# A two-layer graph network on one core: the last expert layer in gapless tiles and visits, and the loop for stray edges moved behind its gates

## The chip, the cores and the metric

The kernel runs on one core of a Trainium2 chip. The time is the device time of one execution in microseconds (us); lower is better. Engines are named as in the profile: PE does matrix products (PEld is its weight load), DVE is the vector engine, ACT the scalar engine, POOL the general engine, whose queue also issues the indirect DMAs (gathers and scatters by a list of row numbers), and SP issues most plain DMAs. Each engine works through its own list of instructions in order and waits for the others by semaphores. DMA transfers run beside them.

## The reference

2500 tokens of 256 values, 40,000 edges, two layers. Each layer adds a graph convolution and an attention part to x and then a mixture of experts. What the change touches is the last step of the second layer:

```python
def _L1_ffn_ref(x, W1, b1, Wg, bg, Wd, bd):        # W1 256x1024, Wg 1024x8, Wd 8x1024x256
    H = gelu(x @ W1 + b1)                            # 2500 x 1024
    probs = softmax(H @ Wg + bg)                     # 2500 x 8
    assign = argmax(probs)
    for e in range(8):
        y = H @ Wd[e] + bd[e]
        out = out + where(assign == e, probs[:, e:e+1] * y, 0)
    return out
...
x = x + gcn(xn, edges) + mix(xn)                     # two convolutions over the edges
x = x + _L1_ffn_ref(layernorm(x), ...)
```

The hidden layer H is the same for all experts. It decides which expert a token belongs to, and only the down-projection Wd differs from expert to expert. Each token goes through one expert alone.

## The kernel before

Tokens lie in X as 20 tiles of 125 rows (X[p, k, :]), five groups of four tiles. A row of X has 256 values and four more: mean, inverse deviation, probability of the chosen expert, and number of the token.

*Convolutions.* The adjacency is written to DRAM once (adj) and is read back in pieces of 219 KB, one hundred over both convolutions, `conv_1` and `conv_2`, through four buffers, all issued by SP in order. For each group, `neighbours` (L288) multiplies 120 times on PE; `conv_2` then transposes the sums (L898) and adds them to X (L901).

*Stray edges.* The adjacency is built for a bounded number of edges per row block. What does not fit would be handled by `lost1`, a loop that runs n_lost times, 0 or 1, known only at run time. On these inputs its body is not run. It stands between conv_2 and the last expert layer, and since it can change X, what reads X comes after it. All five engines meet at it.

*Last expert layer.* Weights (wgf, bgf, b1f, w1, and wd in eight loads of 1 MB) are issued by SP, bdf by ACT. `layernorm_T` computes the statistics of a group (L328 and following), the normalised rows lnt (L361) and their transpose xT (L348). `gates` computes H of the group in eight chunks (L1198), gelu on ACT (L1201) and the logits (L1202); H is then dropped. `route` makes softmax and the chosen expert of each token. `take_slots` gives each token a row in DRAM: every expert has a region of CAP rows in sorted1, fill1 counts how far it is filled. `scatter` (L403) writes the rows of X there, one indirect DMA per tile. The routing of a group is worked off while the next group's chunks run.

After the last group `pad` (L491) writes a tile of empty rows behind each expert's region, and `plan` works out for up to NS1 = 27 tiles of 128 rows which expert they belong to and where they begin. 27 is the number of full tiles in 2500 rows, 20, plus one part tile for seven of the eight experts. Then nine groups of three tiles follow: SP loads the rows (L1243) from an address in a register, DVE normalises (L1247), PE transposes (L1251), DVE and ACT copy to xc (L90, L92), PE computes the hidden layer again on 3456 columns in all (L1257), ACT does gelu (L1259), and for each tile PE multiplies with the expert's wd (L1265, eight calls; the expert's number is a register load, L445). DVE adds the bias (L1269), scales and adds the row (L1270), and POOL writes the rows to out by token number (L1271). Rows that belong to no token have a number out of bounds and are not written.

The order of instructions on an engine is made by a scheduler from the program's order and its dependences, so the order in the code is not always that on the engine.

Of the kernel before, what the change touches and what calls it, by code (L numbers as in the profile page):

```python
# [9 lines left out]
F32 = mybir.dt.float32  # L10
I32 = mybir.dt.int32
# [5 lines left out]
N = 2500  # L17
# [22 lines left out]
NS1 = -(-N // TS) + NE - 1  # L40
# [8 lines left out]
def gps_kernel(ctx: ExitStack, tc: tile.TileContext, a, out):  # L49
# [23 lines left out]
    def mm_tile(p, n):  # L73
        return psum.tile([p, n], F32, tag="mm", name="mm")

    def row_bcast(src, offset, n, p=P):
        return bass.AP(tensor=src.tensor, offset=src.offset + offset, ap=[[0, p], [1, n]])
# [8 lines left out]
    def evacuate(dst, src):  # L86

        flip[0] ^= 1
        if flip[0]:
            S.copy(dst, src)  # L90
        else:
            V.tensor_copy(dst, src)  # L92


    X = xpool.tile([P, NT, RW], F32, tag="X", name="X")
# [25 lines left out]
    slots = const.tile([P, NS0], F32, name="slots")  # L121
# [4 lines left out]
    region = const.tile([P, NE], F32, name="region")  # L126
# [252 lines left out]
    def take_slots(pool, mask, fill):  # L379


        flat = mask.rearrange("p i e -> p (i e)")
        ps = psum2.tile([P, 2, GT, NE], F32, tag="cx", name="ps")
        T.matmul(ps[:, 0].rearrange("p i e -> p (i e)"), below, flat, start=True, stop=True)  # L384
        T.matmul(ps[:, 1].rearrange("p i e -> p (i e)"), ones[:, :P], flat, start=True, stop=True)  # L385
        slot = pool.tile([P, GT, NE], F32, tag="slot", name="slot", bufs=2)
        for k in range(GT):
            V.tensor_tensor(slot[:, k, :], ps[:, 0, k, :], fill, ALU.add)  # L388
            V.tensor_tensor(fill, ps[:, 1, k, :], fill, ALU.add)
        return slot  # L390
# [19 lines left out]
    def plan(pool, fill, ns):  # L410
# [3 lines left out]
        V.tensor_tensor(tiles, fill, region, ALU.subtract)  # L414
# [7 lines left out]
        V.tensor_tensor(of, last[:, None, :].to_broadcast([P, ns, NE]), slots[:, :ns, None].to_broadcast([P, ns, NE]), ALU.is_le)  # L422
# [6 lines left out]
        V.scalar_tensor_tensor(tiles, tiles, -float(TS), region, ALU.mult, ALU.add)  # L429
# [4 lines left out]
        V.scalar_tensor_tensor(who, slots[:, :ns], float(TS), who, ALU.mult, ALU.add)  # L434
        begin = pool.tile([P, ns], I32, name="begin")
        V.tensor_scalar(begin, who, float(NE * CAP), None, ALU.min)
        return expert, begin

# [38 lines left out]
    sorted1 = dram.tile([NE * CAP + TS, RW], F32, name="sorted1")  # L477
    back0 = dram.tile([2 * N, D], F32, name="back0")

    for table in (sorted0, sorted1):  # L480
        nc.scalar.dma_start(table[NE * CAP:NE * CAP + TS, :], empty)

    def pad(pool, table, empty, fill, moved):

        ends = pool.tile([P, NE], I32, name="ends")
        V.tensor_copy(ends, fill)
        made = []
        for e in range(NE):
            r = nc.values_load(ends[0:1, e:e + 1], engines=[mybir.EngineType.SP], min_val=0, max_val=NE * CAP - TS,
                               skip_runtime_bounds_check_because="an expert has at most N tokens")  # L490
            made.append(nc.sync.dma_start(table[ds(r, TS), :], empty))  # L491
            for m in moved + made[:-1]:
                tc.declare_no_dep(made[-1].ins, m.ins, reason="rows of their own")
# [5 lines left out]
    fill0 = const.tile([P, NE], F32, name="fill0")  # L499
    V.tensor_copy(fill0, region)  # L500
    fill1 = const.tile([P, NE], F32, name="fill1")
    V.tensor_copy(fill1, region)
# [633 lines left out]
    with tc.tile_pool(name="lost1", bufs=1) as pool, tc.For_i(0, n_lost, 1):  # L1136
        acc = pool.tile([P, NT, D + 1], F32, name="acc")
        nc.sync.dma_start(acc[:, :, :D], tab1.rearrange("(p k) d -> p k d", p=P))
        V.memset(acc[:, :, D:], 0.0)
        gather_sums(pool, acc, tab1)  # L1140
        tab2 = dram.tile([N, D], F32, name="tab2")
        brow = pool.tile([P, D], F32, name="brow")
        nc.sync.dma_start(brow, row_bcast(a["b1row"], 0, D))
        cT = pool.tile([128, 2, N], F32, name="cT")
        for i in range(NT):
            o = acc[:, i, :D]
            V.scalar_tensor_tensor(o, o, dis[:, i:i + 1], brow, ALU.mult, ALU.add)
            neg = pool.tile([P, D], F32, name="neg")
            V.tensor_scalar(neg, o, 0.0, alpha[:P], ALU.min, ALU.mult)
            V.scalar_tensor_tensor(o, o, 0.0, neg, ALU.max, ALU.add)  # L1150
        for g in range(NG):
            transpose_group(cT, g, lambda k: acc[:, g * GT + k, :D])
        for i in range(NT):
            ps = mm_tile(P, D)
            for c in range(2):
                T.matmul(ps, cT[:, c, i * P:(i + 1) * P], wc2[:, c, :], start=(c == 0), stop=(c == 1))
            V.tensor_scalar(acc[:, i, :D], ps, dis[:, i:i + 1], None, ALU.mult)
        nc.sync.dma_start(tab2.rearrange("(p k) d -> p k d", p=P), acc[:, :, :D])
        gather_sums(pool, acc, tab2)
        for i in range(NT):  # L1160
            V.scalar_tensor_tensor(X[:, i, :D], acc[:, i, :D], dis[:, i:i + 1], X[:, i, :D], ALU.mult, ALU.add)

# [4 lines left out]
    TG = 3  # L1167
    with tc.tile_pool(name="fin", bufs=1) as fin, tc.tile_pool(name="fin2", bufs=2) as fin2:
# [13 lines left out]
        xT = fin.tile([128, 2, N], F32, name="xTf")  # L1182
# [6 lines left out]
        empty = empty_rows(fin)  # L1189
# [17 lines left out]
        def route(g, pl):  # L1207
# [18 lines left out]
            slot = take_slots(fin2, w, fill1)  # L1226
            scatter(sorted1, slot_of(fin2, slot, w), X[:, g * GT:(g + 1) * GT, :], moved)
            yield

        layernorm_T(X, xT, lambda g: fin2.tile([P, GT, D], F32, tag="lnt", name="lnt"), stats=with_row, then=gates)  # L1230
        for _ in range(2):
            next(routing[-1])
        pad(fin, sorted1, empty, fill1, moved)
        expert, begin = plan(fin, fill1, NS1)

        ns = -(-NS1 // TG) * TG
        done = []
        for u in range(ns // TG):
            tiles = range(u * TG, min((u + 1) * TG, NS1))
            nt = len(tiles)  # L1240
            xs = fin2.tile([128, TG, RW], F32, tag="xs", name="xs")
            for k, t in enumerate(tiles):
                nc.sync.dma_start(xs[:, k, :], tile_rows(sorted1, begin, t))  # L1243
            xc = fin2.tile([128, 2, TG * TS], F32, tag="xc", name="xc")
            xh = fin2.tile([128, TG, D], F32, tag="xh", name="xh", bufs=1)
            for k in range(nt):
                V.tensor_scalar(xh[:, k, :], xs[:, k, :D], xs[:, k, D:D + 1], xs[:, k, D + 1:D + 2], ALU.subtract, ALU.mult)  # L1247
            for c in range(2):
                ps = mm_tile(128, TG * TS)
                for k in range(nt):  # L1250
                    T.transpose(ps[:, k * TS:(k + 1) * TS], xh[:, k, c * 128:(c + 1) * 128], ident)  # L1251
                evacuate(xc[:, c, :nt * TS], ps[:, :nt * TS])
            hs = []
            for j in range(nj):
                ps = mm_tile(128, TG * TS)
                for c in range(2):
                    T.matmul(ps[:, :nt * TS], w1[:, c, j * 128:(j + 1) * 128], xc[:, c, :nt * TS], start=(c == 0), stop=(c == 1))  # L1257
                h = fin2.tile([128, TG * TS], F32, tag="hs", name="hs", bufs=12)
                S.activation(h[:, :nt * TS], ps[:, :nt * TS], AF.Gelu, bias=b1f[:, j:j + 1])  # L1259
                hs.append(h)  # L1260
            for k, t in enumerate(tiles):
                e = expert_of(expert, t)
                ps = mm_tile(128, D)
                for j in range(nj):
                    T.matmul(ps, hs[j][:, k * TS:(k + 1) * TS], wd[:, ds(e, 1), j, :], start=(j == 0), stop=(j == nj - 1))  # L1265
                idx = fin2.tile([128, 1], I32, tag="idx", name="idx", bufs=4)
                V.tensor_copy(idx, xs[:, k, D + 3:D + 4])
                yo = fin2.tile([128, D], F32, tag="yo", name="yo", bufs=4)
                V.tensor_tensor(yo, ps, bdf[:, ds(e, 1), :].rearrange("p o n -> p (o n)"), ALU.add)  # L1269
                V.scalar_tensor_tensor(yo, yo, xs[:, k, D + 2:D + 3], xs[:, k, :D], ALU.mult, ALU.add)  # L1270
                done.append(G.indirect_dma_start(  # L1271
                    out=out, out_offset=bass.IndirectOffsetOnAxis(ap=idx, axis=0), in_=yo, in_offset=None,
                    bounds_check=N - 1, oob_is_err=False,
                ))
                for m in done[:-1]:
                    tc.declare_no_dep(done[-1].ins, m.ins, reason="each token has a slot of its own")
# [62 lines left out]
```

## Time and profile before

| what | before |
|---|---|
| median of 3 runs | 2235.64 us (2235.45 to 2235.82) |
| the profiled execution | 2239.74 us, of which its span 2238.0 us |
| PE busy | 2009.1 us, 90% |
| DVE, ACT, POOL busy | 872.0, 594.2, 294.4 us |
| last conv_2 group's products end | 1860.98 us |
| gates, first L1198 to last L1202 | 1877.68 to 1998.51 us |
| last token's row in sorted1 known (L398) | 2005.83 us |
| tiles of experts on PE (L1257 to L1265) | 2022.33 to 2230.45 us |

In the lines of the profile, a group is given as line, engine, operation, output and inputs, shape, and number of instructions, then busy time, mean nanoseconds of one, and the idle time ahead of it with what ended it. In the timeline, the first number is the start in us, the second the length, and in brackets stands how long the engine had been idle and what released it. A row of the slices has one digit for each fortieth of the span, the busy share in tenths.

### The profile page before, as it was taken

What the parts mean: (1) busy time and instruction counts of PE and PEld (TensorE: products, weight loads), DVE (VectorE), ACT (ScalarE), POOL (GpSimd) and SP (SyncE); (2) the same over time, 40 slices, a digit from 0 to 9 for tenths busy, and PEclk for the clock granted to TensorE, in tenths of its full rate; (3) what the DMA queues carried; (4) which work ended last, traced back from release to release, by engine and by line L of the source; (5) the groups of instructions that cost most, each with busy time, mean ns of one, the idle gap of its engine ahead of it and who ended that gap; (6) DMA issues with size and microseconds to landing.
All of it is one profiled execution on the core that took longest, in us unless ns stands there. A gap on an engine that the chain in (4) does not pass through costs nothing. (4 is left out here: it accounts for less than half of the span.)

```text
span 2238.0 us, 25483 instructions
## 1 busy us (share of the span) xinstructions
PE 2009.1 (90%) x9145; PEld 1336.2 (60%) x9145; DVE 872.0 (39%) x2764; ACT 594.2 (27%) x1008; POOL 294.4 (13%) x265
## 2 busy tenths in 40 slices
PE   2799956997799999999999999999987997978998
PEld 2556635876476766676666676767643442326676
DVE  7866532332734463434525463443120003222111
ACT  1533202222533323232233324133110001332221
POOL 2303331222210000100001010011111000120111
PEclk9799977999899999999999999999989998988999
DMA  4113256664410001100110001100025336011110
GB/s 119 37 55 105 78 155 188 206 188 152 105 51 14 1 12 51 42 1 5 45 35 23 1 12 49 47 1 1 1 75 152 86 90 203 19 42 38 31 30 20
DMA packets 87295, 143.51 MB, mean 64 GB/s; under 512 B 18898, under 2 KB 69056, under 8 KB 86402
## 3 DMA queue, kind: packets, MB, share of 16 engines
q1 hardware_dynamic: 71233, 117.01, 18.0%
q0 software_dynamic: 12832, 18.28, 2.9%
q10 hardware_dynamic: 3093, 6.46, 1.1%
q8 instruction: 77, 1.26, 0.2%
q14 instruction: 60, 0.49, 0.1%
HBM read 104.84 MB, written 38.81 MB: 64 GB/s over the span
## 5 line engine op out<-in xcount | busy, mean ns | idle before, releaser
L1089 PE MATMUL mm<-w,h 128*125 128x256 f32 x1280 | 286.1, 379 | 0.0
L1079 PE MATMUL mm<-xT,w 128*128 128x500 f32 x640 | 283.2, 584 | 0.0
L288 PE MATMUL pa<-piece,table 125*128 125x500 bf16 x1200 | 269.8, 378 | 13.5 <-DVE t L852 5.6
L1089 PEld LDWEIGHTS mm<-w,h 128*125 128x125 f32 x1280 | 239.0, 188 | 43.2 <-issue 9.2
L288 PEld LDWEIGHTS <-table 125*128 125x128 bf16 x1200 | 117.7, 99 | 144.5 <-issue 17.8
L1079 PEld LDWEIGHTS mm<-xT,w 128*128 128x128 f32 x640 | 119.3, 191 | 112.6 <-issue 102.2
L1082 ACT ACTIVATE h<-mm,bf 128x500 f32<-128x500 f32 x160 | 107.1, 677 | 231.5 <-PE mm L1079 231.1
L288 PE MATMUL pa<-edges,xb 125*128 125x500 bf16 x600 | 134.2, 377 | 1.7 <-ACT edges L662 1.7
L1074 POOL TENSOR_TENSOR tok<-tok,b 125x1024 f32<-125x1024 f32 x20 | 47.3, 2365 | 584.6 <-DVE tok L1066 534.1
L1090 DVE TENSOR_TENSOR tok<-tok,mm 125x256 f32<-125x256 f32 x80 | 33.5, 418 | 210.0 <-PE mm L1089 169.3
L1257 PE MATMUL mm<-xc,w 128*128 128x384 f32 x288 | 102.1, 511 | 7.5 <-DVE xc L92 5.4
L765 PE MATMUL mm<-xc,wt 128*128 128x128 f32 x752 | 97.1, 283 | 7.5 <-DVE idx L771 4.3
L765 PEld LDWEIGHTS mm<-xc,wt 128*128 128x128 f32 x752 | 89.6, 194 | 17.8 <-DVE xc L761 12.4
L779 PE MATMUL py<-w,h 128*128 x376 | 96.0, 381 | 0.9 <-ACT h L769 0.9
L288 PEld LDWEIGHTS <-xb 125*128 125x128 bf16 x600 | 58.1, 100 | 63.8 <-issue 3.9
L1265 PE MATMUL mm<-wd,hs 128*128 x432 | 94.7, 379 | 0.0
L1055 DVE TENSOR_TENSOR tok<-tok,po 125x256 f32<-125x256 f32 x80 | 30.2, 414 | 154.4 <-PE po L1052 153.9
L769 ACT ACTIVATE h<-mm,wt 128x128 f32<-128x128 f32 x188 | 53.8, 368 | 137.3 <-issue 127.1
L1265 PEld LDWEIGHTS mm<-wd,hs 128*128 128x128 f32 x432 | 82.1, 190 | 13.1
L353 ACT ACTIVATE xT<-mm,mixc 128x500 f32<-128x500 f32 x80 | 58.9, 767 | 114.0 <-PE mm L348 79.8
L662 ACT CAST edges<-mm 125x500 bf16<-125x500 f32 x100 | 64.6, 784 | 88.9 <-PE mm L659 88.9
L1257 PEld LDWEIGHTS mm<-xc,w 128*128 128x128 f32 x288 | 55.4, 198 | 50.9 <-DVE xc L92 10.8
(325 smaller groups left out, 2832.2 us busy)
## 6 DMA issues: line engine op xcount, KB each, us to landing
wt<-in_expert_in_dram SPq DMA_DIRECT2D x47, 514.0 KB
piece<-adj SPq DMA_DIRECT2D x100, 218.8 KB
xs<-sorted SPq DMA_DIRECT2D x74, 130.0 KB
w<-in_L_mix_W_dram SPq DMA_DIRECT2D x8, 1024.0 KB
wd<-in_L_ffn_Wd_dram SPq DMA_DIRECT2D x8, 1024.0 KB
w<-in_L_ffn_W_dram SPq DMA_DIRECT2D x8, 512.0 KB
adj<-edges SPq DMA_DIRECT2D x2, 1750.0 KB
terms<-t SPq DMA_DIRECT2D x10, 336.0 KB
```

The lines of the kernel that those rows point to most:

```text
L288: T.matmul(pa[c], table[:, k, n, c * 128:(c + 1) * 128], e, start=(k == 0 and n == 0), stop=(k == NT - 1 and n == 2))
L353: S.activation(o, ps, AF.Identity, bias=shift[:, c:c + 1], scale=gain[:, c:c + 1])
L662: S.copy(o.rearrange("p s (n d) -> p n s d", d=BD), ps[:P].rearrange("p (n s d) -> p n s d", n=BD, d=BD))
L765: T.matmul(ps[:, j * TS:(j + 1) * TS], wt[:, c * F0 + j * 128:c * F0 + (j + 1) * 128], xc[:, c * TS:(c + 1) * TS], start=(c == 0), stop=(c ...
L769: S.activation(h[:, j * TS:(j + 1) * TS], ps[:, j * TS:(j + 1) * TS], AF.Gelu, bias=wt[:, 2 * F0 + j:2 * F0 + j + 1])
L779: T.matmul(ps, h[:, j * TS:(j + 1) * TS], w2[:, ds(e, 1), j, :], start=(j == 0), stop=(j == NJ - 1))
L1074: G.tensor_tensor(o, o, b2[:P, None, :].to_broadcast([P, GT, D]), ALU.add)
L1079: T.matmul(ps, w1[:, c, j * 128:(j + 1) * 128], fT[:, c, g * GC:(g + 1) * GC], start=(c == 0), stop=(c == 1))
L1082: S.activation(h, ps, AF.Gelu, bias=bf[:, l, j:j + 1])
L1089: T.matmul(ps, hh[j][:, k * P:(k + 1) * P], w2[:, j, :], start=(j == 0), stop=(j == nj - 1))
L1257: T.matmul(ps[:, :nt * TS], w1[:, c, j * 128:(j + 1) * 128], xc[:, c, :nt * TS], start=(c == 0), stop=(c == 1))
L1265: T.matmul(ps, hs[j][:, k * TS:(k + 1) * TS], wd[:, ds(e, 1), j, :], start=(j == 0), stop=(j == nj - 1))
```

## The change

*Gapless tiles.* A token's row is no longer in a region of its expert's own. Two neighbouring experts share N rows: one fills them from the front, the other from the back (begin1, sign, way). sorted1 now lies in the memory of adj, which has been read for the last time by then. `visits` on DVE computes, for 20 gapless tiles of 128 in the order of experts, the row of each place (whence), and for 27 visits the expert, the tile (which), and the tile's place in a ring (kept). A visit is one tile with one expert; a tile in which an expert ends is visited more than once. `fetch` gathers the rows of a tile on POOL into X itself, `turned` normalises and transposes them, `inner` computes the hidden layer of a group of two or four tiles (2500 columns in all) and stores it in a ring of 12 tiles. For each visit, `take` copies the tile's hidden layer (128×1024) from the ring at an address in a register, and `visit` multiplies with the expert's wd. Rows of the tile that belong to another expert get a token number out of bounds (far). `pad` and the row loads on SP go.

*The loop.* `lost1` stands behind the gates. Its body now ends with `sort_all`, which does norm, gates and sort once more, for X has changed.

```diff
-    with tc.tile_pool(name="lost1", bufs=1) as pool, tc.For_i(0, n_lost, 1):
-        ...
     stage.close()
...
-        layernorm_T(X, xT, lambda g: ..., stats=with_row, then=gates)
-        for _ in range(2):
-            next(routing[-1])
-        pad(fin, sorted1, empty, fill1, moved)
-        expert, begin = plan(fin, fill1, NS1)
+        def sort_all():
+            V.tensor_copy(fill1, begin1.rearrange("p k t -> p (k t)"))
+            moved.append([])
+            routing.clear()
+            layernorm_T(X, xT, lambda g: ..., stats=with_row, then=gates)
+            for _ in range(2):
+                next(routing[-1])
+
+        sort_all()
+        with tc.tile_pool(name="lost1", bufs=1) as pool, tc.For_i(0, n_lost, 1):
+            ...
+            sort_all()
+        own, whence, expert, expert_f, which, kept = visits(fin, fill1, at)
...
+            way = fin2.tile([P, GT, NE], F32, tag="way", name="way")
+            V.tensor_tensor(way, w, sign..., ALU.mult)
-            slot = take_slots(fin2, w, fill1)
+            slot = take_slots(fin2, way, fill1)
...
-        for u in range(ns // TG):
-            for k, t in enumerate(tiles):
-                nc.sync.dma_start(xs[:, k, :], tile_rows(sorted1, begin, t))
-            ...
+        hs = fin2.tile([128, RING, nj * TS], F32, name="hs", bufs=1)
+        xs = whole
+        for n in (2, 2, 4, 4, 4, 4):
+            ...
+        def fetch(lo, hi):
+            for t in range(lo, hi):
+                G.indirect_dma_start(out=xs[:m, t, :], out_offset=None, in_=sorted1,
+                    in_offset=bass.IndirectOffsetOnAxis(ap=whence[:m, t:t + 1], axis=0))
+        def take(v):
+            r = nc.values_load(kept[0:1, v:v + 1], engines=[mybir.EngineType.DVE], ...)
+            h = fin2.tile([128, nj * TS], F32, tag="taken", name="taken")
+            V.tensor_copy(h, hs[:, ds(r, 1), :].rearrange("p o n -> p (o n)"))
+            return v, h
+        def visit(v, h):
+            e = expert_of(expert, v)
+            r = nc.values_load(which[0:1, v:v + 1], engines=[mybir.EngineType.DVE], ...)
+            for j in range(nj):
+                T.matmul(ps, h[:, j * TS:(j + 1) * TS], wd[:, ds(e, 1), j, :], ...)
+            row = xs[:, ds(r, 1), :].rearrange("p o n -> p (o n)")
+            V.tensor_scalar(far, own[:, ds(r, 1)], expert_f[:, v:v + 1], float(1 << 20), ALU.not_equal, ALU.mult)
+            V.tensor_tensor(idx, far, row[:, D + 3:D + 4], ALU.add)
+            V.tensor_tensor(yo, ps, bdf[:, ds(e, 1), :]..., ALU.add)
+            V.scalar_tensor_tensor(yo, yo, row[:, D + 2:D + 3], row[:, :D], ALU.mult, ALU.add)
+            G.indirect_dma_start(out=out, ..., in_=yo)
+        fetch(*groups[0])
+        fetch(*groups[1])
+        xc, n = turned(*groups[0])
+        taken = None
+        for u, (lo, hi) in enumerate(groups):
+            inner(lo, hi, xc, n)
+            for v in range(lo, hi if u + 1 < len(groups) else NV):
+                nxt_v = take(v)
+                if taken is not None:
+                    visit(*taken)
+                taken = nxt_v
+                if v == lo and u + 1 < len(groups):
+                    xc, n = turned(*groups[u + 1])
+            if u + 2 < len(groups):
+                fetch(*groups[u + 2])
+        visit(*taken)
```

In the new program the lines have moved: pa is L292, conv_2's transposes and sums L961 and L964, the gates L1237, L1240 and L1241, norm and lnt L332 and L365, the loop L1282, scatter L407, the slots' row numbers L402, fetch L1328, xh L1340, its transposes L1342, inner L1353, gelu L1355, take L1364 and L1367, visit L1373 to L1386.

In the instructions that the scheduler made of it, the norm statistics and lnt of earlier groups stand on DVE between conv_2's groups, and eight lnt transposes and seven of the eighty L1237 products stand on PE there. The weight loads of the last layer (wgf, bgf, b1f, w1, wd, bdf) have left their place behind the loop; on SP they stand in conv_1, between piece loads 32 and 44. On PE, a group's hidden layer, part of the visits and the transposes of the next group but one take turns, and the last twelve visits follow each other.

## The prediction

> **What bounds the kernel now.** First the page's busy shares and slices, then its costliest groups. PE is busy 90% of a span of 2238.0 us, so what counts is where PE stands still and what it does that it need not. The last slices are the stages that the change touches (a slice is 56 us).
>
> ```profile
> PE 2009.1 (90%) x9145; PEld 1336.2 (60%) x9145; DVE 872.0 (39%) x2764; ACT 594.2 (27%) x1008; POOL 294.4 (13%) x265
> ...
> PE   2799956997799999999999999999987997978998
> ...
> L1257 PE MATMUL mm<-xc,w 128*128 128x384 f32 x288 | 102.1, 511 | 7.5 <-DVE xc L92 5.4
> ...
> L1265 PE MATMUL mm<-wd,hs 128*128 x432 | 94.7, 379 | 0.0
> ```
>
> See that the expert stage is PE's own time: 102 us of hidden layer, 95 us of down-projection, 7.5 us of waits between.
>
> Next the timeline around the loop for stray edges, which runs no iteration here.
>
> ```profile
> 1861.81 1.03 PE L898 MATMUL ps<-ident,u 128*125 128x128 f32 x7 [0.38 <-DVE u L92]
> 1862.44 1.66 DVE L901 SCALAR_TENSOR_TENSOR X<-ps,dval,X 125x256 f32<-125x256 f32 x4 [0.69 <-PE ps L898]
> ...
> 1868.70 0.28 DVE L470 MEMSET empty<- 128x260 f32 x1 [4.60 <-issue]
> ...
> 1875.13 1.36 DVE L361 TENSOR_SCALAR lnt<-X,mv,rstd 125x256 f32<-125x256 f32 x4
> ...
> 1875.58 2.06 PE L348 MATMUL mm<-ident,lnt 125*128 125x125 f32 x8 [12.75 <-DVE lnt L361]
> ```
>
> PE stands 12.75 us: DVE is held 4.60 us at the loop, then needs 6.9 us of norm statistics that nothing could start before the loop.
>
> The same view between gates and experts, in three fragments: last logits, last slots and scatters, first hidden tile.
>
> ```profile
> 1997.51 1.00 PE L1202 MATMUL pl<-h,wgf 128*8 128x500 f32 x2 [0.83 <-ACT h L1201]
> ...
> 2005.64 0.19 DVE L398 TENSOR_REDUCE to<-pick 125x4 int32<-125x32 f32 x1
> ...
> 2006.12 1.19 POOL L403 DMA_INDIRECT sorted<-X,to  x1 [7.32 <-DVE tiles L416]
> ...
> 2019.42 0.47 PE L1251 MATMUL mm<-ident,xh 128*128 128x128 f32 x1 [15.63 <-DVE xh L1247]
> ...
> 2022.33 3.93 PE L1257 MATMUL mm<-xc,w 128*128 128x384 f32 x6
> ```
>
> From the last slot (2005.83) to the first hidden matmul is 16.5 us. And one group of three tiles:
>
> ```profile
> 2047.52 9.94 PE L1257 MATMUL mm<-xc,w 128*128 128x384 f32 x30 [0.71 <-DVE xc L92]
> 2057.30 10.52 PE L1265 MATMUL mm<-wd,hs 128*128 x48
> 2067.66 0.82 PE L1251 MATMUL mm<-ident,xh 128*128 128x128 f32 x6
> ```
>
> Fifteen calls (two records each) of 384 columns in 9.94 us are 1.726 ns a column; 24 calls of 256 columns in 10.52 us are 1.712. The stage runs 2022.33 to 2230.45, 208.1 us, and 7.55 us of last output follow.
>
> **The change, part by part.**
>
> *1. The loop leaves the place between conv_2 and gates.* Norm statistics and lnt of the earlier groups now stand between conv_2's groups on DVE, which is idle there while PE does a 25.5 us group (L288); cost nothing, and if that cover failed, the 6.9 us return. In the built order, eight lnt transposes and seven of the eighty L1198 calls also go inside conv_2's four boundaries. A boundary is 2.39 us of which PE works 1.4; what is put in exceeds its idle 1.0 us by 1.05, .75 and .75 us (the fourth nothing), so the last pa ends 1863.5 instead of 1860.98. After it come the last transposes, X (1.66 us) and one lnt group, partly under a remaining L1198; gates resume about 1866.6 with seven calls done (5.9 us at 0.84). Before, gates ran 1877.68 to 1998.51 = 120.8 us; now the end is 1866.6 + 120.8 − 5.9 = 1981.5. The tail to the last slot was 7.3 us, plus .2 for the multiply by the sign: 1989.0 against 2005.83. **Gain 16.8.**
>
> *2. The weight loads.* wgf, b1f, w1 and eight wd (10.5 MB) stood on SP behind the loop. They now go out in conv_1 (about 1625 to 1700 us), between piece loads 32 and 44 of 100 and ahead of term stores. A wd issue cost 2.9 us of SP (four in 11.46), twelve pieces last 30 us on PE (ten per 25.5 us group), and 13 MB in all at the 350 GB/s seen when wd was loaded (1866 to 1876) need 37. Four piece buffers cover 10. Nothing to 8 us; I take 1.5, since 37 − 30 is within the cover.
>
> *3. Start of the experts.* After the last slot: four scatters, 6.1 us as before (2005.83 to 2011.9). Then the loop's barrier waits for them to land. The nearest row is the first loop of the kernel, also behind scatters: last scatter issued 336.38, DVE back 341.40, 5.0 us. Then the new table of visits: 33 small DVE ops, .16 to .38 us each in the rows of the old plan, 7.3 us (the old plan lay under scatters and padding). Then the first gather of rows on POOL: the nearest row, the 125-row gather at L184, took 4.1 us from issue to use; the second 1.5 later. xh, transposes and copies 1.4. Sum 6.1 + 5.0 + 7.3 + 5.6 + 1.5 = 25.5 against 16.5: **loss 9.0.** The padding DMAs (L491, 8.66 us of SP) and the first xs loads go with the old 16.5.
>
> Here a rule speaks against the move. The Trainium skill, "Runtime: NRT & Kernel Launch", section "Instruction fetch mechanics", says that a branch taken to code outside the fetched window stops the engine until a page is fetched. The row: PE's branch at this loop took 3.507 us (3.680 at the first loop), and DVE waited for it. The row at the first loop shows it hidden, because PE came early while the scatters landed; now PE is done ten us before the scatters are. So I take 5.0; by the rule as in the present place another 3.5 to 4.6.
>
> *4. The hidden layer without gaps.* 2500 columns × 16 calls × 1.72 ns = 68.8 us instead of 3456 × 16 × 1.726 = 95.4. Transposes 40 instead of 54, .137 each: 5.5 for 7.4. The 27 visits do the same 27 × 8 × .438 = 94.7 us. PE's sum 169.0. Waits: the first take behind the first gelu 1.5, second group's gather 1, the rest as the .7 at six groups now about .4: 5 in all. 174 against 208.1: **gain 34.**
>
> *5. What each visit adds off PE.* DVE per visit: yo .42 and STT .48 as now; three register loads of .30 (L445; was one); register arithmetic .2; far and idx .2 to .3; and the copy of 128×1024 out of the ring. No such copy is in the trace.
>
> ```profile
> L189 DVE TENSOR_SCALAR fits<-off x4: 220/221/227, 26.1 to 33.6; 125x128 f32<-125x128 f32 x4
> ```
>
> ```profile
> L188 DVE TENSOR_SCALAR off<-win,base x4: 286/287/644, 25.8 to 32.6; 125x128 f32<-125x128 int32 x4
> ```
>
> The Trainium skill, "VectorE: DVE Perf Modes", section "The perf-mode tier table", gives an fp32 copy within SBUF the 2× tier, 1227 ns for 2048 elements, so an estimate of about .65. The rows above agree for 128 elements (.221 with constants, .287 with a per-partition operand), but no row shows a read at an address from a register. Lower bound .65; upper 1.2, by the slope between the per-partition rows of 128 and 256 elements (.287, and .412 at L1247: .98 ns an element, and 896 more); I take .7, since a copy has no per-partition operand. Then a visit costs DVE 3.1 us, under PE's 3.5 a visit. At 1.2 it costs 3.6, and the twelve visits that end the kernel without a hidden layer between them lose up to 2 us.
>
> POOL: twenty gathers at 1.54 us issue and 27 outputs at .97, 57 us in 200, in this order: four gathers, then four outputs. The outputs before a gather read rows of X that the gather overwrites, so a gather waits for them, and DVE's xh for the next group but one waits for its landing with idx and take queued behind. Four gathers take 4 × 1.54 + 2.6 = 8.8 us; meanwhile PE has a hidden group, 16 × .88 = 14 us. Covered by 5 us.
>
> Sum: −16.8 + 9.0 − 34 + 1.5 = −40.3. The profiled execution took 2239.74 with span 2238.0; the new span is 2197.7, and the median of the shown runs lies 4.1 under the profiled time: 2235.64 − 40.3 ≈ **2195**.
>
> **The rivals.**
>
> *DVE (or the chain take, visit, yo) sets the pace.* For it: three register loads and a copy per visit, all in order with xh that waits for gathers. Against: 40 us of DVE work in the 208 now. At 4.2 us a visit instead of 3.5 the 27 visits lose 19 of the gain: about 2214. Chance .14.
>
> *The barrier shows in full.* Branch stall 3.5 to 4.6 plus landing, and register tables 3 us slower: 2203. For it: PE's branch is slow in both loops. Against: PE comes early. Chance .15.
>
> *Better than the sum.* Bubbles near nil and the start in the shadow of shorter landing: 5 + 4 less, 2186. Chance .13.
>
> *Slower than before: gathers serialise with PE.* Place: xh L1340 waiting for gathers that wait for the outputs. Each of the four later groups has 14 us of cover; to lose 41 us they must each come 10 us late beyond it, thus 25 us for four gathers, 5.6 us a gather instead of 1.54 of issue. For it: the row read is chosen at run time, so every read of X is ordered against every gather. Against: L184 shows 1.54. Above 5.6 us a gather, 2236 to 2250. Chance .05.
>
> *The loop move only works.* Visits bound so that gapless tiles bring nothing: −16.8 + 9.0 + 1.5 gives 2229. Against: PE is busy in 96% of the stage now, so removed columns are removed time. Chance .03.
>
> The likeliest, as summed, has .50, 2189 to 2201 on its own.
>
> **How the numbers follow.** A measurement of this kernel tells .2%, 4.5 us, from no change. Slower beyond that .04 (most of the serialising case), same .02 (its edge), faster .94. The range takes in the better case at 2183, the barrier case, and the middle of the DVE case: 2183 to 2213; left out are the slow half of the DVE case (.07), serialising (.05), loop only (.03), and a few hundredths below.
>
> **What would show it.** Part 1: no 12.75 us PE wait before the lnt transposes, conv_2's boundaries 3 to 3.5 us, gates ending 17 us earlier (near 1981). Part 2: PE's wait for piece still near 6 us. Part 3: 25 us from last slot to first L1353; PE's branch long but ended before the scatters land. Part 4: L1353 at 69 us, L1377 at 95, the stage near 174. Part 5: L1367 near .7 us, PE's wait for taken small. The prediction is wrong if PE waits for taken at each visit, if gathers take 5 us, or if conv_1 grows by more than 8.

## The result and the profile after

The changed kernel takes 2200.99 us (four runs, 2194.89 to 2202.26) against 2235.73 before; the ratio is 0.9839, with a 95% interval of 0.9821 to 0.9857. It is 34.7 us faster; 40 were forecast, 2195 in a range of 2183 to 2213.

Single executions of one kernel differ by up to 15 us (2232.17 to 2247.15 for the kernel before in one set of runs), and the difference goes with the clock that TensorE is granted (last section). The profiled execution of the changed kernel is its fastest: 2194.89 us, span 2193.1. The table therefore goes by stages, all in us. The ends are read from the timelines: last product of conv_2, last slot (L398, now L402), first hidden product of the experts, last product, end of the span.

| stage | before | after | difference | forecast |
|---|---|---|---|---|
| start to last product of conv_2 | 1860.98 | 1856.40 | −4.6 | +4.0 |
| to the last slot | 144.85 | 123.52 | −21.3 | −19.3 |
| to the first hidden product | 16.50 | 22.33 | +5.8 | +9.0 |
| to the last product | 208.12 | 181.78 | −26.3 | −34 |
| to the end | 7.55 | 9.07 | +1.5 | 0 |

The last four rows give −40.3 us; the forecast for them was −44.3. In its first row the forecast had 2.5 for products put between conv_2's groups and 1.5 for weight loads. The −4.6 measured there is not shown to be a gain of the change. Two kernels from the experiments below, e1_idx and e8_before_idx, differ from the changed kernel and from the one before only in the stage of the experts; they have 1864.79 and 1855.40 in this row. The lead of the changed kernel was there before conv_2: the last group of conv_1 ended at 1698.23 instead of 1704.14. Half of it is in the two last groups of conv_1, which took 25.49 us each at a granted clock of 1.00; in the profile before they took 26.77 and 27.18 at 0.95 and 0.94. From there to the last product of conv_2 the changed kernel needs 158.2 us instead of 156.8, 1.3 more.

From the page of the changed kernel: the busy shares, the products of both convolutions, and the group that answers to L1265.

```profile
PE 1966.7 (90%) x9035; PEld 1311.6 (60%) x9035; DVE 897.2 (41%) x2822; ACT 580.6 (26%) x989; POOL 315.1 (14%) x288
...
L292 PE MATMUL pa<-piece,table 125*128 125x500 bf16 x1200 | 266.4, 375 | 13.9 <-DMA piece<-adj 10.8
...
L1377 PE MATMUL py<-wd,taken 128*128 x432 | 97.2, 381 | 10.6 <-DVE taken L1367 10.6
```

PE works 42 us less and is still busy 90% of the span. The down-projection, which had no wait before, now waits 10.6 us for `taken`, the copy of a tile's hidden layer.

The timeline of PE where the loop used to stand:

```profile
1856.23 1.00 PE L1237 MATMUL mm<-xTf,w 128*128 128x500 f32 x2
1857.08 1.19 PE L961 MATMUL ps<-ident,u 128*125 128x128 f32 x8
1858.10 1.00 PE L1237 MATMUL mm<-xTf,w 128*128 128x500 f32 x2
1859.04 2.68 PE L1241 MATMUL pl<-h,wgf 128*8 128x500 f32 x6
```

The 12.75 us in which PE stood are gone entirely: products of the gates lie around the last transposes of conv_2.

The timeline between gates and experts: last slot, last scatter, first and last operation of the table of visits, first gather, first hidden product.

```profile
1979.73 0.19 DVE L402 TENSOR_REDUCE to<-pick 125x4 int32<-125x32 f32 x1
...
1984.70 1.19 POOL L407 DMA_INDIRECT adj<-X,to  x1 [0.30 <-DMA adj<-X,to]
1990.65 0.17 DVE L449 TENSOR_TENSOR count<-fill,begin 128x8 f32<-128x8 f32 x1 [10.74 <-issue]
...
1996.20 0.18 DVE L476 TENSOR_TENSOR whence<-place_of,side 128x20 int32<-128x20 f32 x1
1996.65 1.00 POOL L1328 DMA_INDIRECT X<-adj,whence  x1 [10.77 <-DVEq L1373]
...
2002.25 1.22 PE L1353 MATMUL mm<-xc,w 128*128 128x256 f32 x2 [0.25 <-ACT xc L92]
```

From the end of the last scatter's issue (1985.89) to DVE's return at 1990.65 are 4.8 us. PE's branch at the loop is in the view of line L1282 (shortest, median and longest in ns, then first and last start):

```profile
L1282 PEldq COMPARE_BRANCH  x3: 85/187/3333, 1977.1 to 1990.6; - x3
```

The longest of the three is about as long as before (3.3 us, then 3.5). It ran from 1978.2 to 1981.5 and was over while scatters were still being issued.

The timeline of two of the last visits, first DVE and POOL, then PE:

```profile
2152.45 0.48 DVE L1385 SCALAR_TENSOR_TENSOR yo<-yo,X 128x256 f32<-128x256 f32 x1
...
2153.20 0.97 POOL L1386 DMA_INDIRECT out_dram<-yo,idx  x1 [3.89 <-DVE far L1381]
2155.63 0.16 DVE L1382 TENSOR_TENSOR idx<-far,X 128x1 int32<-128x1 f32 x1 [2.58 <-DMA out_dram<-yo,idx]
2155.75 0.42 DVE L1384 TENSOR_TENSOR yo<-py,bdf 128x256 f32<-128x256 f32 x1
2156.69 0.69 DVE L1367 COPY taken<-hs 128x1024 f32 x1 [0.51 <-issue]
```

```profile
2152.59 3.72 PE L1377 MATMUL py<-wd,taken 128*128 x16 [1.14 <-DVE taken L1367]
2157.44 3.72 PE L1377 MATMUL py<-wd,taken 128*128 x16 [1.13 <-DVE taken L1367]
```

A visit comes every 4.85 us where PE has 3.46 us of work. DVE is not busy for most of that: it stands 2.58 us before an operation of 0.16 us, idx, until an output has landed. Behind idx in its queue stand the yo of a visit that PE has finished and the copy for the visit that PE does next (2156.69; PE starts at 2157.44, right behind it). Seven of the last twelve visits begin with such a wait, 8.4 of the 10.6 us.

### The profile page after: what moved, and what is told of

The parts are those of the page before. It is cut to its first block, busy times and chain, and to the rows that moved or that the text cites. A ratio compares the mean times of both kernels' runs of the same rounds, so it can differ in the third digit from the quotient of the medians.

```text
span 2193.1 us, 25312 instructions
## 1 busy us (share of the span) xinstructions
PE 1966.7 (90%) x9035; PEld 1311.6 (60%) x9035; DVE 897.2 (41%) x2822; ACT 580.6 (26%) x989; POOL 315.1 (14%) x288
## 5 line engine op out<-in xcount | busy, mean ns | idle before, releaser
L292 PE MATMUL pa<-piece,table 125*128 125x500 bf16 x1200 | 266.4, 375 | 13.9 <-DMA piece<-adj 10.8
L292 PEld LDWEIGHTS <-table 125*128 125x128 bf16 x1200 | 117.1, 98 | 143.7 <-issue 15.0
L292 PE MATMUL pa<-edges,xb 125*128 125x500 bf16 x600 | 134.4, 377 | 1.7 <-ACT edges L725 1.7
L1377 PE MATMUL py<-wd,taken 128*128 x432 | 97.2, 381 | 10.6 <-DVE taken L1367 10.6
L1377 PEld LDWEIGHTS py<-wd,taken 128*128 128x128 f32 x432 | 81.1, 190 | 26.2 <-DVE taken L1367 14.0
L292 PEld LDWEIGHTS <-xb 125*128 125x128 bf16 x600 | 58.2, 100 | 64.0 <-issue 4.1
L1053 PE MATMUL mm<-xT,wa 128*128 128x500 f32 x160 | 75.5, 614 | 3.7 <-ACT xT L357 3.5
L1115 PE MATMUL po<-gm,qt 128*125 128x256 f32 x320 | 76.5, 382 | 1.9 <-ACT qt L92 1.9
```

The costliest lines, as they stand in the source:

```text
L292: T.matmul(pa[c], table[:, k, n, c * 128:(c + 1) * 128], e, start=(k == 0 and n == 0), stop=(k == NT - 1 and n == 2))
L1053: T.matmul(ps, wk[:, kc, c * 128:(c + 1) * 128], hT[:, kc, g * GC:(g + 1) * GC], start=(kc == 0), stop=(kc == 1))
L1115: T.matmul(po[:, b * D:(b + 1) * D], qt[:, 2 * b + c, :], gm[:, c, :], start=(c == 0), stop=(c == 1))
L1377: T.matmul(ps, h[:, j * TS:(j + 1) * TS], wd[:, ds(e, 1), j, :], start=(j == 0), stop=(j == nj - 1))
```

## Experiments: what holds up the visits

There are four buffers for idx, the row numbers of an output. In the changed kernel DVE waits 30.1 us for outputs before it writes one:

```profile
L1382 DVE TENSOR_TENSOR idx<-far,X 128x1 int32<-128x1 f32 x27 | 3.7, 156 | 34.4 <-DMA out_dram<-yo,idx 30.1 <-DMA X<-adj,whence 4.3
```

The scheduler put the idx of the visit four ahead right behind the present visit's output, and it goes into the buffer that this output was given, so it waits for the landing. yo has four buffers as well and does not wait for outputs: it is written only when its own visit is done. Theory W (waiting) says that the wait of idx costs PE its time; rival B, the prediction's own, says that DVE's work does.

**e1_idx**, the changed kernel with 27 buffers (NV) for idx and far:

```diff
-            idx = fin2.tile([128, 1], I32, tag="idx", name="idx", bufs=4)
-            far = fin2.tile([128, 1], F32, tag="far", name="far", bufs=4)
+            idx = fin2.tile([128, 1], I32, tag="idx", name="idx", bufs=NV)
+            far = fin2.tile([128, 1], F32, tag="far", name="far", bufs=NV)
```

> The changed kernel with a buffer of its own for the idx and far of each visit (27 instead of 4), nothing else. Theory W (waiting): in the visits PE stands for taken because DVE, in order, first waits for an output to land before it may overwrite one of four idx buffers, and yo and take are queued behind. Then the 10.6 us of PE waiting for taken fall to about 3, the last visits come every 3.5 us instead of 4.85, and the time falls by 8 to 10 us, to about 2192. Theory B (DVE's own work for a visit, loads and copy, sets the pace): the work is the same, so the time stays within 2 us of the changed kernel's 2201.

As theory W had it: 2190.99 us, ratio to before 0.9777 (0.9751 to 0.9803), 10 us under the changed kernel. The group of the down-projection, and the last twelve visits in PE's timeline:

```profile
L1377 PE MATMUL py<-wd,taken 128*128 x432 | 95.0, 379 | 0.7 <-DVE taken L1367 0.7
```

```profile
2139.09 41.60 PE L1377 MATMUL py<-wd,taken 128*128 x192
```

These are twelve visits in 41.6 us without a gap, 3.47 each. From first hidden product (2010.58) to last product (2180.69) are 170.1 us instead of 181.8; the granted clock in this stage is 0.98 in both profiles.

**e4_copy2**, e1_idx with the copy made a second time:

```diff
             V.tensor_copy(h, hs[:, ds(r, 1), :].rearrange("p o n -> p (o n)"))
+            V.tensor_copy(h, hs[:, ds(r, 1), :].rearrange("p o n -> p (o n)"))
```

> The same as e1_idx with the copy out of the ring done twice (another 0.69 us of DVE for each of 27 visits). Theory W: DVE then has about 2.8 + 0.7 = 3.5 us of work for a visit of 3.46 us on PE, so 0 to 3 us more than e1_idx. Theory B: each visit is 0.7 us longer, at least in the last twelve, 8 us and up to 19 more than e1_idx.

2189.73 us, ratio 0.9777 (0.9754 to 0.9800), no different from e1_idx; PE waits 0.2 us for taken. With 18.6 us more of copying DVE still keeps up, so rival B is wrong.

**e10_take_act**, four idx buffers as in the changed kernel, but the copy on ACT:

```diff
-            r = nc.values_load(kept[0:1, v:v + 1], engines=[mybir.EngineType.DVE], ...)
-            V.tensor_copy(h, hs[:, ds(r, 1), :]...)
+            r = nc.values_load(kept[0:1, v:v + 1], engines=[mybir.EngineType.Activation], ...)
+            S.copy(h, hs[:, ds(r, 1), :]...)
```

> The changed kernel with four idx buffers as it is, but the copy out of the ring (take) on ACT instead of DVE. It tells which instruction behind the waiting idx costs PE its time. If it is take (theory W as put for e1_idx), PE's wait for taken falls below 3 us though DVE's waits for outputs stay; what is left is the cycle yo, output, landing, idx, yo, near 3.7 us against PE's 3.46, so that the last twelve visits lose some 3 instead of 11 us: 2192 to 2195. If it is yo, whose PSUM tile PE needs back, the time stays at 2200.

2188.74 us, ratio 0.9778 (0.9747 to 0.9808). The groups:

```profile
L1377 PE MATMUL py<-wd,taken 128*128 x432 | 96.7, 381 | 4.1 <-DVE yo L1384 2.8 <-ACT taken L1367 1.1
...
L1382 DVE TENSOR_TENSOR idx<-far,X 128x1 int32<-128x1 f32 x27 | 3.7, 156 | 38.1 <-DMA out_dram<-yo,idx 34.0 <-DMA X<-adj,whence 4.1
```

DVE still waits 34 us for outputs, and PE only 1.1 for taken: the wait costs mainly through the copy queued behind it. What is left, 2.8 us, is yo, whose PSUM tile (PE's output) PE needs back. By itself this run would not tell waiting from work, for DVE also has less to do; e4_copy2 does that. The time came out below the expected 2192 to 2195 and is not to be told from e1_idx (four runs, 2187.36 to 2195.05); in the profiles the stage has 174.9 us against 170.1 in e1_idx.

**e8_before_idx**, the kernel before with 27 idx buffers, meant as a control:

```diff
-                idx = fin2.tile([128, 1], I32, tag="idx", name="idx", bufs=4)
+                idx = fin2.tile([128, 1], I32, tag="idx", name="idx", bufs=27)
```

> The kernel before with 27 buffers for idx in place of 4, as a control. There DVE waits 50.4 us for outputs to land ahead of idx as well, but only yo is behind it, and PE does not wait for yo in a group of three tiles. So the 50 us leave the list of waits and the time stays within 0.2% of before. If idle time of DVE as such cost time, it would be several us faster.

The expectation was wrong: 2228.95 us, ratio 0.9956 (0.9942 to 0.9971), 9.6 us faster. First the group of idx and DVE's queue at the end of a group of three tiles in the kernel before, then what became of it in e8_before_idx: the hidden layer and idx as groups, and one hidden group in PE's timeline.

```profile
L1267 DVE CAST idx<-xs 128x1 int32<-128x1 f32 x27 | 4.0, 153 | 50.7 <-DMA out_dram<-yo,idx 50.4 <-DMA xs<-sorted 0.3
...
2045.93 0.15 DVE L1267 CAST idx<-xs 128x1 int32<-128x1 f32 x1 [2.61 <-DMA out_dram<-yo,idx]
2046.05 0.42 DVE L1269 TENSOR_TENSOR yo<-mm,bdf 128x256 f32<-128x256 f32 x1
2046.52 0.48 DVE L1270 SCALAR_TENSOR_TENSOR yo<-yo,xs 128x256 f32<-128x256 f32 x1
2046.92 0.55 DVE L92 COPY xc<-mm 128x384 f32<-128x384 f32 x1
```

```profile
L1257 PE MATMUL mm<-xc,w 128*128 128x384 f32 x288 | 97.1, 496 | 1.9 <-ACT xc L90 1.9
...
L1267 DVE CAST idx<-xs 128x1 int32<-128x1 f32 x27 | 3.9, 147 | 1.0 <-DMA xs<-sorted 1.0
```

```profile
2040.05 10.59 PE L1257 MATMUL mm<-xc,w 128*128 128x384 f32 x32 [0.24 <-ACT xc L90]
```

In the kernel before, the same wait stood ahead of yo and of DVE's copy to xc at the end of a group. The 0.71 us before L1257 in the fourth view of the prediction, put down to xc, came from there: the copy ends at 2047.47 and PE goes on at 2047.52. Without the wait the hidden layer waits 1.9 us in all instead of 7.5, a group takes 21.84 us instead of 22.8, and the stage 197.5 instead of 208.1. So the wait was not new. It has moved from xc to taken and costs about the same.

## Experiments: the parts of the change

**e2_loop**, the kernel before with the loop alone moved:

```diff
-    with tc.tile_pool(name="lost1", ...), tc.For_i(0, n_lost, 1):      # behind conv_2
+        sort_all()
+        with tc.tile_pool(name="lost1", ...), tc.For_i(0, n_lost, 1):
+            ...
+            sort_all()
         pad(fin, sorted1, empty, fill1, moved[-1])
```

> The kernel before with the loop moved behind the gates alone (its body redoes the sort), tiles and padding as before. By the prediction's steps: 16.8 us gained ahead of the gates, 1.5 lost to weight loads in conv_1; after the last slot the barrier of 5 us stands before the padding (8.7 us of SP), which no longer lies beside the scatters, so 10 to 12 us lost. About 3 to 5 us faster than before, 2231. If the loop's move brings nothing: 2236. The hidden tiles stay at 208 us.

2223.82 us against 2238.70, 0.9932 (0.9912 to 0.9952): 15 us, not 3 to 5. Last product of conv_2 to last slot is 123.3 us (−21.6), last slot to first hidden product 25.7 (+9.2). The loss is near the 10 to 12 that were expected; the gain ahead of the last slot had been put too low, and the weight loads bring no loss (e11_loads).

**e3_tiles**, the changed kernel with the loop back in its old place:

```diff
+    with tc.tile_pool(name="lost1", ...), tc.For_i(0, n_lost, 1):      # behind conv_2, body as before
     stage.close()
...
         sort_all()
-        with tc.tile_pool(name="lost1", ...), tc.For_i(0, n_lost, 1):
-            ...
```

> The changed kernel with the loop back in its old place between conv_2 and the gates (its body as before), gapless tiles and visits kept. The stage of the visits then shows what it showed in the changed kernel, 183 us for 208, and the start after the last slot has no barrier: visits beside the scatters, 16 to 17 us. About 25 us faster than before, 2210, the weight loads back behind the loop. If tiles and move help each other (additive parts do not hold), e2_loop and e3_tiles together differ from the changed kernel's 35 us by more than 5.

2216.86 us, 0.991 (0.9888 to 0.9932): 21.8 us faster than before. The visits take 183.0 us and the start after the last slot 14.9. The two parts sum to 36.7 us, the whole change has 34.7: within the scatter they add.

**e11_loads**, the kernel before with the weight loads alone put ahead of the loop:

```diff
+        # wgf, bgf, b1f, bdf, w1, wd loads here
         with tc.tile_pool(name="lost1", ...), tc.For_i(0, n_lost, 1):
```

> The kernel before with one thing changed: the weight loads of the last layer (wgf, bgf, b1f, w1, wd, bdf) stand ahead of the loop, so that SP issues them in conv_1 among its piece loads, as in the changed kernel. It prices the prediction's step 2. As predicted: 1.5 us slower, PE's waits for piece at the head of conv_2 2 to 3 us longer. If the loads also hold PE's products in conv_1 up (the groups of 120 products of conv_1 then take 27.2 us instead of 25.5 in most executions): 4 to 8 us slower. If they are hidden: within 1 us, since behind the loop PE waits for lnt and not for weights.

2236.48 us (14 runs) against 2237.63 (19), 0.9990 (0.9980 to 1.0001): the loads are hidden. PE at the head of conv_2, three lines of the kernel before and two of e11_loads:

```profile
1717.26 2.06 PE L288 MATMUL pa<-piece,table 125*128 125x500 bf16 x9 [3.39 <-DVE t L852]
1721.02 7.76 PE L288 MATMUL pa<-piece,table 125*128 125x500 bf16 x36 [1.70 <-DMA piece<-adj]
1732.64 16.86 PE L288 MATMUL pa<-piece,table 125*128 125x500 bf16 x72 [3.86 <-DMA piece<-adj]
...
1719.94 9.50 PE L288 MATMUL pa<-piece,table 125*128 125x500 bf16 x36 [6.71 <-DMA piece<-adj]
1730.46 17.90 PE L288 MATMUL pa<-piece,table 125*128 125x500 bf16 x84 [1.02 <-DMA piece<-adj]
```

It waits 7.7 us for pieces, in place of 5.6 for pieces and 3.4 for t before: the pieces come later, but the wait for t is gone.

**e7_wdlate**, e1_idx with wd held back to conv_2:

```diff
+            V.tensor_copy(wd[:P, e, 0, 0:1], X[:, 0, 0:1])
             nc.sync.dma_start(wd[:, e], a["L1_ffn_Wd"][e]...)
```

> e1_idx with the eight loads of wd (8 MB) held back until conv_2's first group is done (each waits for a one-column copy from X into its tile); SP then issues them among conv_2's piece loads. If the loads in conv_1 make pieces late (8.6 + 2.2 us of PE waiting for piece at the head of conv_2 against 5.6 before), those waits fall to about 5 and the time by 2 to 5 us, 2187. If they cost nothing, within 2 us of e1_idx; if pieces in conv_2 become late instead, more than e1_idx.

2185.07 us, 0.9761 (0.9728 to 0.9794). Its interval overlaps that of e1_idx, and e11_loads shows no cost of the loads, so the 6 us are not shown to be a gain of the edit. Its profile speaks against one: the waits for pieces at the head of conv_2 fall to 4.6 us as expected, but 3.4 for t come back, 8.0 in all against 8.6 in e1_idx.

**e6_noloop**, e1_idx without the loop (stray edges are left out):

```diff
-        with tc.tile_pool(name="lost1", ...), tc.For_i(0, n_lost, 1):
-            ...
```

> e1_idx without the loop for stray edges after the gates; it leaves out the handling of edges that do not fit, which these inputs do not have. It prices the barrier: with it, 10.7 us pass from the last slot to DVE's first table operation; without it the table lies beside the scatters and the first gather waits only for their landing, as in e3_tiles (14.9 us from last slot to first hidden product). 7 to 8 us under e1_idx, 1 to 2 under e5_table. If PE's branch of 3.3 us were exposed, e5_table would be 4 to 5 us above this kernel.

2185.83 us, 0.9758 (0.9726 to 0.9791): 5 us under e1_idx, not 7 to 8. The first gather goes out 3.8 us after the last scatter is issued (1994.13 to 1997.93). Until then DVE, whose table is done, waits for the scatters to land:

```profile
1997.56 0.21 DVE L1354 TENSOR_SCALAR far<-own,expert_f 128x1 f32 x1 [3.85 <-DMA adj<-X,to]
```

From last slot to first hidden product are 15.5 us.

**e5_table**, e1_idx with the table computed ahead of the loop:

```diff
         sort_all()
+        visits(fin2, fill1, at, table_of)
         with tc.tile_pool(name="lost1", ...), tc.For_i(0, n_lost, 1):
             ...
             sort_all()
-        own, whence, ... = visits(fin, fill1, at)
+            visits(fin2, fill1, at, table_of)
```

> e1_idx with the table of visits computed at the end of the sort, ahead of the loop (and again in the loop's body, into the same tiles). If the start of the experts is set by DVE's chain of barrier, then 33 table operations, then gather, the 5.7 us of the table fall beside the scatters and the barrier: from the last slot to the first hidden product 16.6 us instead of 22.3, the time 5 to 6 us under e1_idx, about 2185. If the gather has to wait for something else (landing of scatters), less than 3 us.

2186.42 us, 0.9756 (0.9720 to 0.9791); by the totals alone it is not shown to be faster than e1_idx. The gain is read from the stage: last slot to first hidden product is 17.3 us, 5.0 less than in e1_idx, and the first gather follows the last scatter by 5.9 us. Against e6_noloop's 3.8, the loop itself costs about 2 us here, less than the 3.3 us of PE's branch in the changed kernel; the rest of the barrier is landing that has to be waited for anyway.

**e9_all**, e1_idx, e5_table and e7_wdlate together.

> e1_idx, e5_table and e7_wdlate together: 27 buffers for idx and far, the table ahead of the loop, wd loaded during conv_2. If the three do not touch each other, 2191 less 5 and 6: about 2180, 58 us or 2.6% under the kernel before. If late wd loads were only worth something because of an execution with a better clock in conv_1, 2184 to 2186.

2183.16 us (2178.97 to 2185.60), 0.9747 (0.9721 to 0.9773): the lowest median, 18 us under the changed kernel. Its stage of visits has 170.2 us and its start 17.6. It lies between the two expectations and is not shown to be faster than e5_table.

## Why the prediction was right, and where it was not

*Part 1, the loop and the norm, forecast 16.8 gained: mechanism right, size too low.* Net of what goes between conv_2's groups it was near 21. The boundaries were to grow by .75 to 1.05 us each, by what is put in over PE's idle 1.0. The distance of two groups' starts grew from 27.88 us (1751.83 to 1779.71) to 28.04 (1774.84 to 1802.88), by 0.16 (0.27 at the first boundary), as the products fill the waits for u and X that stood between the transposes. And no lull was left ahead of the last gates, where about 3 us had been allowed.

*Part 2, the weight loads, forecast 1.5 lost: nothing within the measurement (e11_loads).* The sign named for it did not come: PE's wait for pieces at the head of conv_2 was 10.8 us in the changed kernel, not near 6. It replaces 9.0 us of waiting for t and pieces, so little of it is a loss.

*Part 3, the start, forecast 9.0 lost: 5.8.* The barrier was 4.8 us (5.0 taken from the first loop). The case in which PE's branch shows, to which the rule on taken branches in the Trainium skill, "Runtime: NRT & Kernel Launch", section "Instruction fetch mechanics", pointed, did not come: the branch took 3.3 us, but beside the scatters, as the row of the first loop said. That it waited for instructions no run here shows. The table took 5.7 us, not 7.3, as many of the 33 operations overlap; the gather was usable after 3.5 us instead of 4.1, and its transposes followed at once.

*Part 4, the hidden layer, forecast 34 gained: 26.3.* The sum of PE's work was right. By the prediction's own rates it falls from 197.5 us (95.4 + 94.7 + 7.4) to 169.0, by 28.5. The two kernels without the wait of idx, e8_before_idx and e1_idx, have stages of 197.5 and 170.1 us, 27.4 apart. What went wrong is the time beside the work. The forecast let the 10.6 us by which the old stage exceeded 197.5 shrink to 5, without asking what made xc late; they stayed, as 12.8 of the new stage's 181.8.

The step that failed is in part 5, "what each visit adds off PE". It summed DVE's operations to 3.1 us (its terms give 2.9 to 3.0), under PE's 3.5, and stopped there. The copy was .69 us, near the .7 taken and the estimate of .65 from the Trainium skill, "VectorE: DVE Perf Modes", section "The perf-mode tier table", and e4_copy2 shows that DVE could do it twice. What the sum left out is a wait: idx before the landing of an output. The kernel before had it, 50.4 us of idle DVE time ahead of L1267, and it was passed over as idle time of an engine that does not bound. Since take was added to the same queue, the question had to be what now stands behind that wait.

*The rivals.* The one in which DVE sets the pace, chance .14, had the right place and the right sign and the wrong cause: 4.85 us in the last visits by waiting, not by work. Gathers that serialise did not occur: each took about 1 us to issue, and PE's transposes waited for a gather only at the start of the stage; the hidden groups covered the others. That the loop's move alone works is ruled out by e3_tiles.

That the total of 40.3 lay so near 34.7 is partly luck. The gain of part 1 was forecast 4 us too small and the loss of part 3 about 3 too large, the gain of part 4 nearly 8 too large, and these errors cancel.

## What to carry to other kernels

In both kernels here, a buffer that was given to an output DMA was held until the DMA had landed, even one with a single word a partition. List such buffers, see where the scheduler puts the next write to each, and ask what stands behind it in that queue; 27 buffers for idx instead of 4 were worth 10 us in both kernels. An idle time in the profile of an engine that does not bound is harmless only as long as nothing that the bounding engine needs is put behind it.

## What was not expected of the hardware

*An output's landing.* In the visits an indirect output of 128 rows let DVE go on about 1.5 us after its issue ended (2154.17 to 2155.63). The four scatters of 125 rows, each row four values longer, kept the gather waiting 3.8 us in e6_noloop.

*The clock.* The spread within each kernel goes with the mean clock that TensorE was granted. The kernel before ran 48 times beside the experiments; its runs average 2244 us at a clock of 0.953, 2239 at 0.955 and 2234 at 0.959. Part of the difference is in conv_1: of two like groups of 120 products in the profile of e8_before_idx, one took 25.49 us at a granted clock of 1.00 and the other 27.18 at 0.94. From 1620 to 1720 the granted clock was 0.91 in the profile of the changed kernel and 0.86 in that of e1_idx. The four runs of the changed kernel lie 34 to 40 us below the averages of the kernel before at the same clocks, so the change may be worth a little more than the 34.7 of the medians. What sets the clock stays open; the early weight loads do not show in it, since e11_loads left the time as it was.
